# Attention values by seven block products, with a passage through DRAM to put them in order

## The chip, the cores and the metric

The kernel runs on one core of one Trainium2 chip. The metric is the device time of one execution in microseconds (us). Before the change the median of three runs is 2184.22 us (2183.15 to 2187.87).

## The reference

The input x has 2048 rows of 256 numbers. It is normalized by row, and the output is x plus an attention over 16 heads plus a gated feed-forward part whose weights are rounded to -1, 0 and 1. Everything is in 32-bit floats. What matters here is the attention:

```python
xn = _layernorm(x, axis=-1)
qkv = einsum('bsd,ed->bse', xn, Wqkv).reshape(B, S, 3 * H, D)   # H = 16, D = 128, S = 2048
q, k, v = qkv[:, :, :H], qkv[:, :, H:2 * H], qkv[:, :, 2 * H:]
logits = einsum('bqhd,bkhd->bhqk', q, k) * D ** (-0.5)
w = softmax(logits, axis=-1)
out = einsum('bhqk,bkhd->bqhd', w, v).reshape(B, S, H * D)
return einsum('bse,de->bsd', out, Wout)
```

## The kernel before

TensorE (PE) multiplies, ScalarE (ACT) takes the exponentials, VectorE (DVE) finds the maxima and reads products out of PSUM, GpSimd (POOL) does additions and subtractions in SBUF and issues part of the transfers; SyncE (SP) issues most of the others.

The normalized input lies transposed in SBUF as `xnT` (128 x 2 x 2048: two halves d of the 256 features, 2048 rows in four chunks of QB = 512). A loop over u goes through blocks of one head and 512 queries. There are 16 heads with NB = 4 blocks each, in 8 groups of G = 2 heads, so a group has GB = 8 blocks. Each block has TB = 4 quarters t of 128 queries. This text calls a pair of block i in its group and quarter t the slot (i,t); blocks 0 to 3 belong to the group's first head, 4 to 7 to its second; (8,t) is (0,t) of the next group. All engines carry out their instructions in the order in which the code issues them, so the place of a call in the loop is its place in each engine's queue.

In a slot, in order of issue, PE computes 128 x 2048 scores `s` for the query block that lies LEAD = 6 slots ahead (`scores`, in halves of 64 columns by `in_halves`, L94), then one product "beside" it (into the one PSUM bank of `ps_m`), then the weighted values of the current block (`weighted`, L716), and then, if the slot has one, a second product into the same bank. DVE reads the first product in the same slot, behind the maxima `mx`; it reads the second at the start of the next slot (`left`), behind the additions of weighted values to `oU` (`added`, L742, L746). In t = 2 and 3 of the running block the products are the block products for queries and keys of a later head (`pw`); in t = 0 and 1 they are output products of the group before (`pow`) while i < 4, and values of the group to come (`pvw`) while i >= 4. Before the change a value product (`v_product`) is 8 matmuls of 256 columns into one bank, for 256 rows of both heads, and there is no second product; `v_read` copies it with two DVE copies, rows in the partitions.

Queries and keys already come from seven products instead of eight: `weight_sums` and `x_sums` make sums of weight blocks and of chunks of x, `fast_product` multiplies them and `fast_read` combines the results. The chunks are taken in pairs, (0,1) and (2,3); `ts[0]` and `ts[2]` hold the four differences of a pair.

The weighted values too use fewer products. The exponentials are exchanged between partitions by DMA (`part<-p`), transposed by DVE into slots of `R` (`transposed`, L649), and POOL makes four differences T1 to T4 of them (`differences`, L669), some in halves: T1b and T3b at the start of t = 0, T2l at its end, T2h and T4 in t = 1, T1a and T3a of the next block in t = 3. `weighted` runs over k in four passes, one in each quarter: pass 0 in t = 0 takes `R` as it came, pass 1 takes T1 and T2 (T2l holds k < 4, T2h k >= 4), pass 2 T3, pass 3 T4, with half as many matmuls. The values have sums as well: `v_combined(h, 0)` and `(h, 1)` make two parts of `st` in the slot before a head's first block, `(h, 2)` and `(h, 3)` the others in its slot t = 1.

POOL's queue at the boundary of two blocks is: T1a and T3a (t = 3), `v_combined` 0 and 1 where a head begins, `put_away` (od<-oU, L772, waits for the finished `oU`), T1b, the transfer of the reciprocals (oT<-rd, L626), T3b, T2l, what `between` adds, T2h, T4. In t = 2 it issues rd<-r (L620). `between(n, t)` stands at the end of each slot and issues loads and transfers.

Of the kernel before, what the change touches and what calls it, by code (L numbers as in the profile page):

```python
# [9 lines left out]
F32 = mybir.dt.float32  # L10
F32R = mybir.dt.float32r
AF = mybir.ActivationFunctionType
ALU = mybir.AluOpType
# [7 lines left out]
def layernorm_attention_bitffn_kernel(  # L21
# [14 lines left out]
    nc = tc.nc  # L36
    P = 128
    S, DM = x.shape
    FF = w1T.shape[1]
    D = P  # L40
    HD = woutT.shape[0]
    H = HD // D
    KC = DM // P
    QB = 512
    NB = S // QB
    TB = QB // P
    NKT = S // P
# [3 lines left out]
    G = 2  # L51
# [18 lines left out]
    weights = {}  # L70
# [19 lines left out]
    def in_halves(out, lhs, rhs, start, stop, both=(True, True)):  # L90

        for c in range(2):
            if both[c]:
                nc.tensor.matmul(  # L94
                    out[c * HP : (c + 1) * HP], lhs[:, c * HP : (c + 1) * HP], rhs,
                    start=start, stop=stop, skip_group_check=True,
                )
# [47 lines left out]
    def weight_sums(h: int):  # L145
# [6 lines left out]
        nc.gpsimd.tensor_tensor(w[:, 3], wk[:, 1], w[:, 1], sub)  # L152
        ws[h] = w

    def x_sums(c: int):
        t = apool.tile([P, 4, QB], F32, tag=f"t{c}", name=f"t{c}", bufs=1)
        x00, x10 = (xnT[:, d, bass.ts(c, QB)] for d in range(KC))
        x01, x11 = (xnT[:, d, bass.ts(c + 1, QB)] for d in range(KC))
        for i, (a, b) in enumerate(((x01, x00), (x11, t[:, 0]), (x11, x01), (x10, t[:, 1]))):
            nc.gpsimd.tensor_tensor(t[:, i], a, b, ALU.subtract)  # L160
        ts[c] = t

    def fast_product(h: int, b: int, i: int, second: bool):

        c = b // 2 * 2
        wk, wq = (weights[h // G, i][:, :, bass.ts(h % G, D)] for i in "kq")
        w, t = ws[h], ts[c]
        x00, x10 = (xnT[:, d, bass.ts(c, QB)] for d in range(KC))
        x11 = xnT[:, 1, bass.ts(c + 1, QB)]
        lhs, rhs = {  # L170
            (0, 0): ((wk[:, 0], x00), (w[:, 1], t[:, 1])),
            (0, 1): ((w[:, 2], t[:, 2]), (wq[:, 1], t[:, 3])),
            (1, 0): ((w[:, 0], t[:, 0]), (w[:, 3], x11)),
            (1, 1): ((wk[:, 1], x10),),
        }[b % 2, i][second]
        pm = ps_m.tile([P, QB], F32, tag="m", name=f"pw{h}_{b}_{i}_{int(second)}")
        in_halves(pm, lhs, rhs, True, True)
        return pm

    def fast_read(h: int, b: int, i: int, second: bool, pm):  # L180
        c = b // 2 * 2
        if (b % 2, i) == (0, 0):
            if not second:
                if c == 0:
                    kTs[h] = kvpool.tile([P, S], F32, tag="kT", name=f"kT{h}")
                for j in range(2):
                    qTs[h, c + j] = kvpool.tile(
                        [P, QB], F32, tag="qT", name=f"qT{h}_{c + j}", bufs=NB + 2
                    )
        k0, k1 = (  # L190
            kTs[h].rearrange("p (j k r) -> p k j r", j=P // 32, r=32)[:, j * TB : (j + 1) * TB]
            for j in (c, c + 1)
        )
        q0, q1 = qTs[h, c], qTs[h, c + 1]
        pk = pm.rearrange("p (k j r) -> p k j r", j=P // 32, r=32)
        def q_sum(q, base):
            nc.vector.tensor_tensor(q, pm, base, ALU.add)  # L197

        def k_sum(k, base):
            nc.vector.tensor_tensor(k, pk, base, ALU.add)  # L200

        if (b % 2, i) == (0, 0):
            if not second:
                nc.vector.tensor_copy(k0, pk)
            else:
                k_sum(k1, k0)
        elif (b % 2, i) == (0, 1):
            if not second:
                nc.vector.tensor_tensor(
                    q1.rearrange("p (k j r) -> p k j r", j=P // 32, r=32), pk, k1, ALU.add  # L210
                )
            else:
                q_sum(q0, q1)
        elif (b % 2, i) == (1, 0):
            if not second:
                q_sum(q1, q1)
            k_sum(k1, k1)
        else:
            k_sum(k0, k0)
# [24 lines left out]
    def v_tile(h: int):  # L244

        if h == 1:
            return osums.rearrange("p b e (k d) -> p (b e k) d", d=D)
        if h not in vs:
            vs[h] = kvpool.tile([P, NKT, D], F32, tag="v", name=f"v{h}", bufs=3)
        return vs[h]  # L250
# [7 lines left out]

    def v_product(g: int, m: int, second: bool):
        w = weights[g, "v"]
        pm = ps_m.tile([P, 2, G * D], F32, tag="m", name=f"pvw{g}_{m}")
        for j in range(2):
            for d in range(KC):
                in_halves(
                    pm[:, j], xnT[:, d, bass.ts(2 * m + j, P)], w[:, d], d == 0, d == KC - 1
                )
        return pm

    def v_read(g: int, m: int, second: bool, pm):
        for j in range(G):
            nc.vector.tensor_copy(
                v_tile(g * G + j)[:, 2 * m : 2 * m + 2], pm[:, :, bass.ts(j, D)]
            )

    ppool = ctx.enter_context(tc.tile_pool(name="ppool", bufs=2))
    front = ExitStack()
# [7 lines left out]
    ods = [  # L286
        [away.tile([P, G, QB], F32, tag=f"od{g}_{c}", name=f"od{g}_{c}") for c in range(NB)]
        for g in range(2)
    ]
    rds = [away.tile([P, 32], F32, tag=f"rd{i}", name=f"rd{i}") for i in range(2)]  # L290

# [393 lines left out]
    def v_combined(h: int, i: int):  # L685
        ((l11, l12), (l21, l22)), st, s3 = v_parts(h)
        o, x, y, op = (
            (st[:, 0], l21, l22, ALU.add), (st[:, 1], st[:, 0], l11, ALU.subtract),
            (s3, l11, l21, ALU.subtract), (st[:, 2], l12, st[:, 1], ALU.subtract),
        )[i]  # L690
        nc.gpsimd.tensor_tensor(o, x, y, op)
# [87 lines left out]
    def o_fetched(g: int, b: int):  # L779
        nc.gpsimd.dma_start(o3, ods[g % 2][b])  # L780
# [86 lines left out]
    GB = G * NB  # L867
# [7 lines left out]
    def between(n: int, t: int):  # L875

        g, i = divmod(n, GB)
        last = NBK - NB

        if t == 1:  # L880
            if i == NB - 1 and g + 1 < H // G:
                load_weights(g + 1, "v", nc.gpsimd)
            elif i == GB - 1 and n < last or n == last - 1:
                load_weights(g, "o", nc.gpsimd)
        if g and i < NB:
            if t == 0 and i + 1 < NB:
                y_moved(i + 1, False)
            elif t == 1 and i + 1 < NB:
                o_fetched(g - 1, i + 1)
        elif n < last:  # L890
            if (i, t) == ((GB - 2, 2) if g else (GB - 1, 2)):
                y_moved(0, False)
            if (i, t) == (GB - 2, 3):
                o_fetched(g, 0)
        if n >= last - 1 and t == (1 if n < last else 2):
            b = n + 1 - last
            nc.gpsimd.dma_start(o3[:, b % 2], ods[(H - 2) // G % 2][b][:, 0])
        if (n, t) in ((last - 2, 3), (last - 1, 2)):
            fetched_back(n + 2 - last)
        if t == 0 and n in (last - 3, last - 2, last, last + 1):  # L900
            x_fetched((last - 3, last - 2, last, last + 1).index(n))

    behind = []
    with tc.manual_schedule():
        for u in range(-LEAD, (NBK - 1) * TB):
# [13 lines left out]
            if n >= NB and t < 2:  # L919
                i, j = divmod(i, NB)  # L920
                j = 2 * j + t
                if not i:
                    seven, hi = True, (g - 1, j)
                    product, read, twice = o_product, o_read, False
                elif g + 1 < H // G:
                    seven, hi = True, (g + 1, j)
                    product, read, twice = v_product, v_read, False
            pms = []

            def beside():  # L930
# [10 lines left out]
            if t == 0 and n >= 0:  # L941
                if 0 < n <= NBK - NB:
                    put_away(n - 1)
                differences(n, "T1b")
                spread(n)
                differences(n, "T3b")
            elif t == 1 and n >= 0:
                differences(n, "T2h")
                if blocks[n][1] == 0:
                    v_combined(blocks[n][0], 2)  # L950
                    v_combined(blocks[n][0], 3)
                differences(n, "T4")
            elif t == 3 and -1 <= n < NBK - 2:
                differences(n + 1, "T1a")
                if n % GB < NB <= n < NBK - NB - 2:
                    y_moved(n % GB, True)
                differences(n + 1, "T3a")
                if n >= 0 and blocks[n + 1][1] == 0:
                    v_combined(blocks[n + 1][0], 0)
                    v_combined(blocks[n + 1][0], 1)  # L960
            if more:
# [117 lines left out]
```

## Time and profile before

| | before |
|---|---|
| median of three runs | 2184.22 us |
| profiled execution | 2184.97 us |
| its span | 2183.2 us |
| PE busy, share of the span | 2160.2 us, 99% |
| DVE | 1725.5 us, 79% |
| ACT | 1374.6 us, 63% |
| POOL | 1472.0 us, 67% |
| granted PE clock, mean | 0.998 |
| value products pvw on PE | 896 matmul records, 117.7 us |
| block products pw<-t,ws on PE | 336 matmul records, 105.3 us |
| value copies on DVE (L273) | 112 of 128x256, 417 ns each |
| transfers of 512 KB by POOL, to landing | o<-od 4.2, osums<-yd 4.3, yd<-osums 3.4, ya<-in_x_dram 6.3 us |

Times in the views are us from the start of the span. Busy times leave out DMA-issuing instructions. The span of 2183.2 us and the time of the profiled execution differ by 1.8 us. A PE instruction of the program appears as two matmul records, and the two halves of 64 columns run side by side, so that lengths on PE are best read from the start of one stretch to the start of the next. In the timeline a line merges equal instructions that follow each other; in brackets stands the idle time before and what ended it.

### The profile page before, as it was taken

Reading aid. Unit: us, or ns where it says so; the run is one execution under the profiler, and the core shown is the slowest. Engines: PE = TensorE matmul, PEld = TensorE weight load, DVE = VectorE, ACT = ScalarE, POOL = GpSimd, SP = SyncE. Lnnn points to the kernel's source line nnn. Section 1 sums busy time; section 2 is a strip of 40 time slices with the busy share of each in tenths; the row PEclk is TensorE's granted clock in tenths of the full one; section 3 lists DMA queues with packets and bytes.
Section 4 is the critical chain, followed back from the end, with each engine's and each line's share of the span. In section 5 each row is a group of like instructions: output and inputs, shape, how many; then the busy total and the mean of one; then the engine's idle time right before and its main releaser. Section 6 shows DMA issues by size and latency. Waiting matters only on the chain. (4 is left out here: it accounts for less than half of the span.)

```text
span 2183.2 us, 41234 instructions
## 1 busy us (share of the span) xinstructions
PE 2160.2 (99%) x14074; PEld 1412.8 (65%) x14074; DVE 1725.5 (79%) x2338; ACT 1374.6 (63%) x2414; POOL 1472.0 (67%) x884
## 2 busy tenths in 40 slices
PE   9998999999999999999999999999999999999998
PEld 6744567776666666666666666666666665666665
DVE  6567887888887887888788788788788878888774
ACT  5586666666666666666666666666666666666662
POOL 0067767767667766767777776786766777677772
PEclk9999999999999999999999999999999999999999
DMA  2155545665556655566555654566555665556652
GB/s 93 41 115 138 124 112 136 159 170 134 120 138 164 163 129 124 142 170 156 122 135 143 175 144 113 135 159 172 130 118 138 173 160 126 126 141 175 168 144 80
DMA packets 180771, 300.65 MB, mean 138 GB/s; under 512 B 54416, under 2 KB 59920, under 8 KB 180560
## 3 DMA queue, kind: packets, MB, share of 16 engines
q1 hardware_dynamic: 127472, 174.69, 31.7%
q0 software_dynamic: 27152, 88.30, 15.9%
q10 hardware_dynamic: 25936, 35.03, 6.4%
q8 instruction: 111, 1.82, 0.4%
q14 instruction: 100, 0.82, 0.1%
HBM read 61.93 MB, written 34.54 MB: 44 GB/s over the span
## 5 line engine op out<-in xcount | busy, mean ns | idle before, releaser
L669 POOL TENSOR_TENSOR R<-R 128x1024 f32<-128x1024 f32 x441 | 1176.6, 2679 | 115.5 <-DVE R L649 100.4
L94 PE MATMUL s<-kT,qT 128*64 128x512 f32 x4000 | 953.2, 593 | 2.1 <-ACT p L578 2.1
L605 ACT COPY part<-p 32x512 f32<-32x512 f32 x1024 | 630.7, 616 | 394.8 <-issue 269.9
L568 DVE TENSOR_REDUCE mx<-s 128x1 f32<-128x1024 f32 x512 | 620.6, 1222 | 300.7 <-PE s L94 287.1
L94 PEld LDWEIGHTS s<-kT,qT 128*64 128x64 f32 x4000 | 502.9, 137 | 308.5 <-issue 80.9
L578 ACT ACTIVATE p<-s,nm 128x1024 f32<-128x1024 f32 x512 | 565.9, 1110 | 209.1 <-PE pw L94 105.7
L649 DVE STREAM_TRANSPOSE R<-part 128x1024 f32<-128x1024 f32 x512 | 605.2, 1220 | 15.1 <-DMA part<-p 13.1
L716 PE MATMUL av<-R,v 128*64 128x256 f32 x3728 | 551.0, 379 | 0.1
L716 PE MATMUL av<-R,st 128*64 128x256 f32 x3024 | 471.7, 379 | 11.0 <-POOL R L669 9.0
L716 PEld LDWEIGHTS av<-R,v 128*64 128x64 f32 x3728 | 363.4, 137 | 160.3 <-issue 8.8
L716 PEld LDWEIGHTS av<-R,st 128*64 128x64 f32 x3024 | 304.2, 137 | 97.3 <-POOL R L669 13.0
L620 POOL DMA_DIRECT2D rd<-r x60 | 33.7, 562 | 233.9 <-DVE r L619 233.9
L734 ACT COPY oU<-av 64x256 f32<-64x256 f32 x248 | 90.7, 366 | 127.0 <-PE av L716 124.6
L772 POOL DMA_DIRECT2D od<-oU x60 | 34.0, 567 | 195.1 <-DVE oU L746 192.6
L742 DVE TENSOR_TENSOR oU<-av,oU 64x256 f32<-64x256 f32 x248 | 102.2, 412 | 45.5 <-ACT oU L734 42.8
L94 PE MATMUL pvw<-wv,xnT 128*64 128x256 f32 x896 | 117.7, 379 | 0.0
L94 PE MATMUL pow<-o,wo 128*64 128x512 f32 x448 | 116.1, 592 | 0.0
L94 PEld LDWEIGHTS pvw<-wv,xnT 128*64 128x64 f32 x896 | 78.6, 137 | 42.3 <-DVE qT L197 5.2
L94 PE MATMUL pw<-t,ws 128*64 128x512 f32 x336 | 105.3, 592 | 0.0
L578 ACT ACTIVATION_READ_ACCUMULATOR p<-s,nm 128x1 f32 x512 | 100.3, 196 | 0.0
L94 PEld LDWEIGHTS pow<-o,wo 128*64 128x64 f32 x448 | 58.9, 137 | 37.3 <-issue 5.4
L200 DVE TENSOR_TENSOR kT<-pw,kT 128x512 f32<-128x512 f32 x112 | 76.9, 686 | 1.7
(146 smaller groups left out, 1332.2 us busy)
## 6 DMA issues: line engine op xcount, KB each, us to landing
part<-p SPq DMA_DIRECT2D x2552, 64.0 KB, 2.2
part<-p ACTq DMA_DIRECT2D x520, 64.0 KB, 2.1
oT<-rd POOLq DMA_DIRECT2D x60, 256.0 KB, 5.6
od<-oU POOLq DMA_DIRECT2D x60, 256.0 KB, 2.7
o<-od POOLq DMA_DIRECT2D x28, 512.0 KB, 4.2
osums<-yd POOLq DMA_DIRECT2D x28, 512.0 KB, 4.3
yd<-osums POOLq DMA_DIRECT2D x26, 512.0 KB, 3.4
yd<-yT SPq DMA_DIRECT2D x4, 512.0 KB, 2.6
```

The costliest lines, as they stand in the source:

```text
L94: nc.tensor.matmul(out[c * HP : (c + 1) * HP], lhs[:, c * HP : (c + 1) * HP], rhs, start=start, stop=stop, skip_group_check=True,)
L200: nc.vector.tensor_tensor(k, pk, base, ALU.add)
L568: nc.vector.tensor_reduce(mx[:, i : i + 1], s, AX.X, ALU.max)
L578: nc.scalar.activation(p, s, AF.Exp, bias=nm, scale=SCALE, accum_out=sums[n][:, t, i : i + 1],)
L605: nc.scalar.copy(*ends(j, j))
L620: nc.gpsimd.dma_start(rds[n % 2], riT)
L649: nc.vector.transpose(to[:, t % 2, 2 * i : 2 * i + 2], part.rearrange("p g (s c) -> p g s c", s=2),)
L669: nc.gpsimd.tensor_tensor(o, x, y, ALU.subtract)
L716: nc.tensor.matmul(av[i * HP : (i + 1) * HP, half], l[:, kk], moving(s, kk), start=start, stop=(k == units[r] - 1), skip_group_check=True,)
L734: nc.scalar.copy(u[op, oq], av[ap, half])
L742: nc.vector.tensor_tensor(u[p, q], av[p, half], u[p, q], ALU.add)
L772: nc.gpsimd.dma_start(ods[h // G % 2][b][:, h % G], oU)
```

## The change

The values of the groups 1 to 7 are made by seven block products for each half of the rows, in the way of the queries and keys. The two heads of the group take the places of query and key weights. `v_sums` makes four sums of weight blocks on POOL. `fast_v_product` gives 2 products of 512 columns in each slot with t = 0 or 1, i >= 4, but one in (5,1) and (7,1): 14 in a group. `fast_v_read` combines them on DVE: 16 operations on 128 x 512.

The results have features in the partitions and have to be transposed. For each head and half (1024 rows) `v_sent` writes 512 KB to DRAM in one transfer, `v_landed` brings it back in one, in pieces of 1 KB and with its blocks of 32 partitions exchanged, into a part of `xnT`, and `v_transposed` turns the 32 x 32 blocks by two DVE transposes of 512 elements a partition. `v_steps` puts these into `between`. For the part of `xnT` to be free, the chunks of the second pair change their parts: `pair(2)` is (3, 2) instead of (2, 3), in the products of queries and keys too.

`v_combined` 0 and 1 of a group's first head move from their place after T3a in (7,3) to the end of that slot, behind the last `v_transposed`.

```diff
+    def pair(c: int):
+        return (c, c + 1) if c == 0 else (c + 1, c)
+
     def x_sums(c: int):
         t = apool.tile([P, 4, QB], F32, tag=f"t{c}", name=f"t{c}", bufs=1)
-        x00, x10 = (xnT[:, d, bass.ts(c, QB)] for d in range(KC))
-        x01, x11 = (xnT[:, d, bass.ts(c + 1, QB)] for d in range(KC))
+        c0, c1 = pair(c)
+        x00, x10 = (xnT[:, d, bass.ts(c0, QB)] for d in range(KC))
+        x01, x11 = (xnT[:, d, bass.ts(c1, QB)] for d in range(KC))
...
-    def v_product(g: int, m: int, second: bool):
...
-    def v_read(g: int, m: int, second: bool, pm):
...
+    def v_sums(g: int):
+        wv = weights[g, "v"]
+        sums_of(wv[:, :, D:], wv[:, :, :D], f"wvs{g}")
+
+    def sums_of(k, q, name: str):
+        w = wpool.tile([P, 4, D], F32, tag="wx", name=name)
+        nc.gpsimd.tensor_tensor(w[:, 0], q[:, 0], q[:, 1], ALU.add)
+        nc.gpsimd.tensor_tensor(w[:, 1], w[:, 0], k[:, 0], ALU.subtract)
+        nc.gpsimd.tensor_tensor(w[:, 2], k[:, 0], q[:, 0], ALU.subtract)
+        nc.gpsimd.tensor_tensor(w[:, 3], k[:, 1], w[:, 1], ALU.subtract)
+        wxs[name] = w
+
+    def fast_v_product(g: int, m: int, second: bool):
+        half, m = divmod(m, NB)
+        wv, w, t = weights[g, "v"], wxs[f"wvs{g}"], ts[2 * half]
...
+        lhs, rhs = (
+            ((wv[:, 0, D:], x00), (w[:, 1], t[:, 1])),
+            ((w[:, 2], t[:, 2]), (wv[:, 1, :D], t[:, 3])),
+            ((w[:, 0], t[:, 0]), (w[:, 3], x11)),
+            ((wv[:, 1, D:], x10),),
+        )[m][second]
+        pm = ps_m.tile([P, QB], F32, tag="m", name=f"pvw{g}_{half}_{m}_{int(second)}")
+        in_halves(pm, lhs, rhs, True, True)
         return pm
...
+    def fast_v_read(g: int, m: int, second: bool, pm):
...
+        if (m, second) == (0, False):
+            nc.vector.tensor_copy(k0, pm)
+            return
+        todo = {
+            (0, True): ((k1, k0),), (1, False): ((q1, k1),), (1, True): ((q0, q1),),
+            (2, False): ((q1, q1), (k1, k1)), (2, True): ((k1, k1),), (3, False): ((k0, k0),),
+        }[m, second]
+        for o, i in todo:
+            nc.vector.tensor_tensor(o, pm, i, ALU.add)
+
+    def v_sent(h: int, half: int):
+        v = v_half(h, half).rearrange("p k d -> p (k d)")
+        nc.gpsimd.dma_start(
+            vds[h % G][half].rearrange("(r q) x -> q r x", q=P // 32), v
+        )
+
+    def v_landed(h: int, half: int):
+        nc.gpsimd.dma_start(landing, vds[h % G][half].rearrange("p (j c) -> j p c", j=P // 32))
+
+    def v_transposed(h: int, half: int):
+        v = v_half(h, half).rearrange("p k (q r) -> p q k r", r=32)
+        w = landing.rearrange("p (q k r) -> p q k r", q=P // 32, r=32)
+        for u in range(2):
+            nc.vector.transpose(v[:, 2 * u : 2 * u + 2], w[:, 2 * u : 2 * u + 2])
+
+    wxs, landing = {}, xnT[:, 0, QB : 3 * QB]
...
     def between(n: int, t: int):
...
+        v_steps = {
+            (5, 1): [(v_sent, 0, 0)], (5, 2): [(v_landed, 0, 0)],
+            (5, 3): [(v_transposed, 0, 0), (v_sent, 1, 0)],
+            (6, 1): [(v_landed, 1, 0)], (6, 2): [(v_transposed, 1, 0)],
+            (7, 1): [(v_sent, 0, 1)], (7, 2): [(v_landed, 0, 1)], (7, 3): [(v_transposed, 0, 1)],
+            (8, 1): [(v_sent, 1, 1)], (8, 2): [(v_landed, 1, 1)], (8, 3): [(v_transposed, 1, 1)],
+        }
...
+        for late in range(2):
+            if late < g + 1 < H // G + late:
+                for do, j, half in v_steps.get((i + late * GB, t), ()):
+                    do((g + 1 - late) * G + j, half)
+        if t == 3 and i == GB - 1 and g + 1 < H // G:
+            v_combined((g + 1) * G, 0)
+            v_combined((g + 1) * G, 1)
...
+        if t == 3:
+            if i == NB - 1 and g + 1 < H // G:
+                v_sums(g + 1)
...
-                    product, read, twice = v_product, v_read, False
+                    product, read, twice = fast_v_product, fast_v_read, j % NB != NB - 1
...
-                if n >= 0 and blocks[n + 1][1] == 0:
+                if n >= 0 and (n + 1) % GB == NB:
                     v_combined(blocks[n + 1][0], 0)
                     v_combined(blocks[n + 1][0], 1)
```

More of the change, by code (lines that the diff above doesn't have):

```diff
@@ L167, in fast_product @@
         w, t = ws[h], ts[c]
-        x00, x10 = (xnT[:, d, bass.ts(c, QB)] for d in range(KC))
-        x11 = xnT[:, 1, bass.ts(c + 1, QB)]
+        c0, c1 = pair(c)
+        x00, x10 = (xnT[:, d, bass.ts(c0, QB)] for d in range(KC))
+        x11 = xnT[:, 1, bass.ts(c1, QB)]
         lhs, rhs = {
@@ L191, in fast_read @@
             kTs[h].rearrange("p (j k r) -> p k j r", j=P // 32, r=32)[:, j * TB : (j + 1) * TB]
-            for j in (c, c + 1)
+            for j in pair(c)
         )
-        q0, q1 = qTs[h, c], qTs[h, c + 1]
+        q0, q1 = (qTs[h, j] for j in pair(c))
         pk = pm.rearrange("p (k j r) -> p k j r", j=P // 32, r=32)
@@ L255, in v_place @@
         return (k + NKT // 2) % NKT if h == 1 else k
-    def v_product(g: int, m: int, second: bool):
[L262 to L268, printed above, removed]
-        return pm
-    def v_read(g: int, m: int, second: bool, pm):
-        for j in range(G):
-            nc.vector.tensor_copy(
-                v_tile(g * G + j)[:, 2 * m : 2 * m + 2], pm[:, :, bass.ts(j, D)]
-            )
+    def v_sums(g: int):
+        wv = weights[g, "v"]
+        sums_of(wv[:, :, D:], wv[:, :, :D], f"wvs{g}")
@@ new lines, in sums_of @@
+    def sums_of(k, q, name: str):
[8 more added lines that the diff above has]
+        wv, w, t = weights[g, "v"], wxs[f"wvs{g}"], ts[2 * half]
+        c0, c1 = pair(2 * half)
+        x00, x10 = (xnT[:, d, bass.ts(c0, QB)] for d in range(KC))
+        x11 = xnT[:, 1, bass.ts(c1, QB)]
+        lhs, rhs = (
[6 more added lines that the diff above has]
+        in_halves(pm, lhs, rhs, True, True)
+        return pm
@@ new lines, in v_half @@
+    def v_half(h: int, half: int):
+        return v_tile(h)[:, half * NKT // 2 : (half + 1) * NKT // 2]
+    def fast_v_read(g: int, m: int, second: bool, pm):
+        half, m = divmod(m, NB)
+        q, k = (
+            v_half(g * G + i, half).rearrange("p k d -> p (k d)").rearrange(
+                "p (j k r) -> p k j r", j=P // 32, r=32
+            )
+            for i in range(G)
+        )
+        k0, k1, q0, q1 = (
+            i[:, j % 2 * TB : (j % 2 + 1) * TB] for i in (k, q) for j in pair(2 * half)
+        )
+        pm = pm.rearrange("p (k j r) -> p k j r", j=P // 32, r=32)
+        if (m, second) == (0, False):
[7 more added lines that the diff above has]
+            nc.vector.tensor_tensor(o, pm, i, ALU.add)
@@ new lines, in v_sent @@
+    def v_sent(h: int, half: int):
+        v = v_half(h, half).rearrange("p k d -> p (k d)")
+        nc.gpsimd.dma_start(
+            vds[h % G][half].rearrange("(r q) x -> q r x", q=P // 32), v
+        )
+    def v_landed(h: int, half: int):
[5 more added lines that the diff above has]
+            nc.vector.transpose(v[:, 2 * u : 2 * u + 2], w[:, 2 * u : 2 * u + 2])
@@ L288, in layernorm_attention_bitffn_kernel @@
         for g in range(2)
+    ]
+    vds = [
+        [away.tile([P, S // 2], F32, tag=f"vd{h}{i}", name=f"vd{h}{i}") for i in range(2)]
+        for h in range(G)
     ]
```

## The prediction

> **What bounds the kernel now.** I read the page first: its span, the busy time by engine, and the chain that ended last.
>
> ```profile
> span 2183.2 us, 41234 instructions
> PE 2160.2 (99%) x14074; PEld 1412.8 (65%) x14074; DVE 1725.5 (79%) x2338; ACT 1374.6 (63%) x2414; POOL 1472.0 (67%) x884
> PE 1%; DVE 0%; issue 0%; ACTq 0%; ACT 0%; DVEq 0%
> ```
>
> PE is busy for 99% and the chain names only the tail, so the set time is the matmul stream, provided it never waits. The busy time by engine of block 6 of one group (it begins at 907 us) confirms it: PE is busy for all of its 32.71 us, as it is in blocks 4, 5, 7 and 8.
>
> ```profile
> core 0: us, PE busy (x) PEld busy (x) DVE busy (x) ACT busy (x) POOL busy (x), PEclk, DMA share, GB/s
> 1100.40:1133.11 32.71, 32.71 (x228) 21.52 (x226) 26.65 (x36) 21.38 (x39) 23.20 (x16) 1.00 0.54 136
> ```
>
> So a saved matmul is worth its full time, and so is every wait the change makes for PE. The waits of PE say who comes closest:
>
> ```profile
> PE av L716 <- POOL R L669: 9.0, 8, 3.3
> ```
>
> Next, the PE timeline. A slot (i,t) is block i of the group, quarter t; (8,0) is (0,0) of the next group. Slots (6,1), (6,3) and (7,0):
>
> ```profile
> 1112.45 2.10 PE L94 MATMUL pvw<-wv,xnT 128*64 128x256 f32 x16
> 1114.17 3.82 PE L716 MATMUL av<-R,st 128*64 128x256 f32 x32
> ...
> 1126.23 3.80 PE L94 MATMUL s<-kT,qT 128*64 128x512 f32 x16
> 1129.66 1.23 PE L94 MATMUL pw<-t,ws 128*64 128x512 f32 x4
> 1130.52 2.10 PE L716 MATMUL av<-R,v 128*64 128x256 f32 x16
> 1132.25 1.23 PE L94 MATMUL pw<-t,wq 128*64 128x512 f32 x4
> ...
> 1136.54 2.10 PE L94 MATMUL pvw<-wv,xnT 128*64 128x256 f32 x16
> 1138.27 3.82 PE L716 MATMUL av<-R,v 128*64 128x256 f32 x32
> ```
>
> Lengths are taken from start to start: scores 3.43 (1126.23 to 1129.66), a value product 1.73 (1136.54 to 1138.27), one block product pw 0.86 (1129.66 to 1130.52), weighted values 1.73 in t=3 and twice that elsewhere.
>
> **What PE saves.** Per group 8 value products of 1.73 become 14 block products, whose shape is that of pw: 13.84 - 14 x 0.86 = **1.80 us**, or 12.6 us in 7 groups. Nearly all of it falls in (5,1) and (7,1), where there is no second product. But the product ahead of the weighted values falls from 1.73 to 0.86 in every slot with t=0 or 1, and the second one stands behind them: those matmuls now come **0.87 us earlier in their slot**.
>
> **What this meets on POOL.** The weighted values of t=1 read in their first half (k<4) what difference T2l writes, and in their second half, 1.73 us later, what T2h writes. Both end a POOL chain that starts when DVE has finished the previous block's oU. Block 6:
>
> ```profile
> 1103.07 0.69 DVE L746 TENSOR_TENSOR oU<-oU,oT 128x512 f32<-128x512 f32 x1
> 1104.05 0.56 POOL L772 DMA_DIRECT2D od<-oU  x1 [3.92 <-DVE oU L746]
> 1112.37 2.35 POOL L669 TENSOR_TENSOR R<-R 128x1024 f32<-128x1024 f32 x1
> ```
>
> The od issue starts 0.29 us after oU ends at 1103.76; T2h (third line) ends at 1114.72. PE needs it at 1114.17 + 1.73 = 1115.90. A slack of 1.18 us becomes 0.31 by the 0.87 above. In block 4 T2h ends at 1050.2 for a need at 1051.36: 1.16 becomes 0.29. In blocks 5 and 7 the slack is about 2 us and stays above 1. In block 8 the o product (1.73) stays, and the slack is 0.57 us (need 1180.45, T2h ends at 1179.88). A POOL end reaches PE after some 0.09 us: in (2,1) of the same group T2h ended at 986.88 and PE, which waited, went on at 986.97.
>
> Now the additions, each where it stands, per group.
>
> *v_sums in (3,3).* Four 128x128 additions on POOL, like the four ws (1119.32 to 1121.13, 1.81 us), just ahead of the od issue of (4,0), which has 0.86 us of idle time before it. So od and T2h come 0.95 us late: 0.95 - 0.29 + 0.09 = **0.75 us** of PE wait in (4,1).
>
> *v_transposed in (5,3).* Two transposes of 512 elements on DVE. Two of 1024 take 2.36 us (below), so I take half of it with an end overhead: 1.22. Its transfer back, issued at about 1093.7 behind rd, has until 1102.5. DVE does not idle between there and the reads of (6,0):
>
> ```profile
> 1100.21 2.36 DVE L649 STREAM_TRANSPOSE R<-part 128x1024 f32<-128x1024 f32 x2
> 1102.60 0.43 DVE L742 TENSOR_TENSOR oU<-av,oU 64x256 f32<-64x256 f32 x1
> 1103.79 2.36 DVE L568 TENSOR_REDUCE mx<-s 128x1 f32<-128x1024 f32 x2
> ```
>
> The first read of (6,0), now 0.68 us, starts at 1106.31 + 1.22 and ends at 1108.21; the second product, due at 1100.40 + 3.44 + 0.86 + 3.46 = 1108.16, waits 0.14 for the one bank. od and T2h are late by 1.22: 1.22 - 0.31 - 0.14 + 0.09, about 0.8 us in (6,1). Together **0.95 us**.
>
> *v_transposed in (6,2).* Its v_landed stands on POOL behind T4 and ws, so with the 1.22 it is issued at about 1122.3. DVE has done its own transposes at 1126.60 + 0.95 = 1127.55. The transfer is 512 KB from DRAM in 1 KB pieces; the rows are
>
> ```profile
> osums<-yd POOLq DMA_DIRECT2D x28, 512.0 KB, 4.3
> ...
> ya<-in_x_dram POOLq DMA_DIRECT2D x4, 512.0 KB, 6.3
> ```
>
> between 4.3 (long pieces) and ya's largest, 7.6. I take 6.3, because ya has the same size, queue and piece length. Then it lands at 1128.6, DVE waits 1.1 us and transposes to 1129.9, and behind it are queued two oU additions (0.85) and the read of (6,2)'s second product (0.61), on which the first product of (6,3) waits: due at 1130.6, it starts at 1131.5 (0.9 us). Maxima and read follow; the second product, only 1.73 us behind here, waits 0.55 more. **1.45 us**. If it lands by 4.3, 0.25 us is left (that slot has almost no slack now: its read ends at 1132.14, the product starts at 1132.25); at 7.6, 2.75.
>
> [...]
>
> *v_transposed and v_combined in (7,3).* Two st sums (2.63 us with their gap) move on POOL from before DVE's end of block 7 to behind the transposes; od follows:
>
> ```profile
> 1164.65 1.27 POOL L691 TENSOR_TENSOR st<-v 128x512 f32<-128x512 f32 x1
> 1166.00 1.28 POOL L691 TENSOR_TENSOR st<-st,v 128x512 f32<-128x512 f32 x1
> 1168.61 0.58 POOL L772 DMA_DIRECT2D od<-oU  x1 [1.33 <-DVE oU L746]
> ```
>
> DVE ends its transposes at 1167.1, and v's at 1168.35; the sums run to 1171.1, and od starts there instead of at 1168.61: 2.5 us late. 2.5 - 0.57 + 0.09, about **2.05 us** in (8,1).
>
> *Without a term of their own.* The other v_landed of (7,2) and (8,2) are issued some 8 us ahead of the transposes. The v_sent (0.56 us each, as yd) stand in POOL's idle time ahead of rd (3 to 6 us), except in (5,3) and (8,1), where od (idle 3.9) and rd follow late enough; without that cover each would put 0.56 on od. v_landed in (8,2) waits for v_sent's landing and holds T1a 1.3 us, which has until (9,1). The 14 more DVE reads (16 of about 0.61 us for 16 of 0.34) fall in t=1 and 2, where DVE idles over 2 us, or in (5,0) and (7,0), where they still end before the second product. The (8,3) transposes take (9,1)'s slack of 1.4 us down to about 0.2. The exchange of the second pair's parts adds no instruction.
>
> [...]
>
> **Sum.** Waits 0.75 + 0.95 + 1.45 + 2.05 = 5.20 us; less 1.80: **+3.40 us per group**, +23.8 in 7. The profiled execution was 2184.97 us (span 2183.2 and 1.8 around it) and would become 2208.8; from the median of 2184.2 I get **2208.0 us**.
>
> **Rivals.** *The POOL and DVE chains have room that I misjudge* (they start earlier where PE has waited, and the waits vanish): the product saving alone stands, 2184.2 - 12.6 = 2171.6. For it: PE loses nothing today. Against: the slacks of 0.3 and 0.57 us are read from the trace. It decides from the point where all waits stay under 1.8 us per group, less than the one in (8,1). Chance 0.12. *Only (8,1) waits:* 2.05 - 1.80 = +0.25 per group, 2186. It needs v_sums and both transposes hidden. 0.06. *The transfers crowd the exchange of the parts:* the queues are 52 to 54% busy in these blocks, and each half adds 1 MB. If every one of the 28 returns lands 2 us later still, past DVE's arrival, that is 28 x 1 to 2 us more: 2236 and above. Against: blocks 0 to 3 carry three such transfers each and PE never waits for a part there. 0.12.
>
> **Range and chances.** The forecast has 0.70. Its own bounds: with half of the waits (2.6) +0.8 per group, 2190; with the slow landing (+1.3) and a 1 us wait at another one, +5.7, 2224. That leaves out the first rival, the crowding one and part of the second, about 0.2. What a measurement can tell from no change is 0.2%, 4.4 us. Faster 0.12, same 0.06, slower 0.82.
>
> **What would show it.** PE busy falls by about 12 us, yet its waits for POOL R grow from 9 to 30 us or so, most in (8,1), whose slot goes from 8.60 to about 10.7; (4,1) and (6,1) to 9.4; (6,3) from 6.88 to 8.3; (5,1) and (7,1) fall to 7.75. v_landed lands in about 6.3. It is wrong if those slots stay at 8.60, or if (6,3) shows no wait of DVE for a transfer.

## The result, and the profile after

The changed kernel takes 2530.67 us (median of 5 runs, 2525.63 to 2537.83) against 2186.08 us before on the same chip: a ratio of 1.1577, 95% interval 1.1555 to 1.1599. The sign of the forecast was right; its size of 1% was not: the loss is 345 us, more than fourteen times the 23.8 forecast.

The page of the changed kernel, with the rows of the transfers that the prediction had to size:

```profile
span 2536.1 us, 40375 instructions
PE 2229.6 (88%) x13570; PEld 1253.6 (49%) x13570; DVE 1794.4 (71%) x2394; ACT 1378.2 (54%) x2414; POOL 1554.3 (61%) x968
vd<-v POOLq DMA_DIRECT2D x28, 512.0 KB, 11.5
xnT<-vd POOLq DMA_DIRECT2D x28, 512.0 KB, 12.9
yd<-osums POOLq DMA_DIRECT2D x26, 512.0 KB, 3.4
ya<-in_x_dram POOLq DMA_DIRECT2D x4, 512.0 KB, 5.9
```

The last column is the median time from issue to landing. The sending, which the prediction likened to yd (3.4 us) without writing down a landing of its own, takes 11.5; the return, which it put beside ya (6.3), takes 12.9. The rows it compared with have hardly moved: yd 3.4 as before, ya 5.9 for 6.3, osums 5.0 for 4.3. The waits, each with who waited for whom, the total, the count and the longest:

```profile
DVE v L335 <- DMA xnT<-vd: 290.8, 28, 14.7
PE av L783 <- DVE oU L809: 110.4, 14, 8.8
PE pow L94 <- DVE qT L202: 103.2, 7, 15.5
PE pw L94 <- DVE kT L205: 57.8, 7, 9.9
PE av L783 <- POOL R L736: 16.0, 22, 3.3
```

The first line is the cause and the next three are its effects on PE: every one of the 28 `v_transposed` (L335) stands on DVE waiting for its return, 10.4 us on average, and PE waits for what is queued behind it. One such place is (6,0). The three views show first POOL, then DVE, then PE:

```profile
1237.18 0.75 POOL L324 DMA_DIRECT2D vd<-v  x1
1242.81 0.57 POOL L687 DMA_DIRECT2D rd<-r  x1 [4.88 <-DVE r L686]
1250.24 1.61 POOL L329 DMA_DIRECT2D xnT<-vd  x1 [6.87 <-DVE kT L205]
```

```profile
1250.72 2.37 DVE L716 STREAM_TRANSPOSE R<-part 128x1024 f32<-128x1024 f32 x2 [0.72 <-DMA part<-p]
1262.09 1.30 DVE L335 STREAM_TRANSPOSE v<-xnT 128x512 f32<-128x512 f32 x2 [9.01 <-DMA xnT<-vd]
1263.43 0.43 DVE L809 TENSOR_TENSOR oU<-av,oU 64x256 f32<-64x256 f32 x1
```

```profile
1255.26 1.03 PE L94 MATMUL pvw<-xnT,wv 128*64 128x512 f32 x4
1263.91 6.25 PE L783 MATMUL av<-R,v 128*64 128x256 f32 x32 [7.62 <-DVE oU L809]
1269.99 1.02 PE L94 MATMUL pvw<-t,wvs 128*64 128x512 f32 x4
```

The sending leaves at 1237.18. The return is next in POOL's queue behind rd and goes out at 1250.24, 13.1 us after the sending. The view puts the 6.87 us of idle time before it down to DVE, but the sending's last 4 KB packet ends only at 1249.28: it is the landing of vd that ends there. The return lands at about 1262.1; DVE waits 9.01 us, and only then adds the weighted values that free PE's bank. PE waits 7.62 us.

Slot lengths, taken from the starts of the scores on PE, say where the time stands. The numbers are means of groups 1 to 6; all other slots keep their length within 0.1 us:

| slot | before | after | difference |
|---|---|---|---|
| (4,1), (8,1) | 8.64, 8.60 | 9.29, 9.40 | +0.65, +0.80 |
| (4,3), (8,3) | 6.91, 6.88 | 7.10, 7.10 | +0.18, +0.22 |
| (5,1), (7,1) | 8.61 | 7.75 | -0.87 each |
| (6,0) | 8.61 | 20.56 | +11.95 |
| (6,3) | 6.88 | 17.74 | +10.87 |
| (8,0) | 8.60 | 19.17 | +10.56 |
| (9,0) | 8.60 | 25.76 | +17.16 |

Together +50.6 us per group, 354 in 7, close to the difference of the two spans (352.9). Each of the four returns costs one slot 10.6 to 17.2 us.

### The profile page after: what moved, and what is told of

Same layout as the page of the kernel before. It is cut to its first block, busy times and chain, and to the rows that moved or that the text cites. A ratio compares the mean times of both kernels' runs of the same rounds, so it can differ in the third digit from the quotient of the medians.

```text
span 2536.1 us, 40375 instructions
## 1 busy us (share of the span) xinstructions
PE 2229.6 (88%) x13570; PEld 1253.6 (49%) x13570; DVE 1794.4 (71%) x2394; ACT 1378.2 (54%) x2414; POOL 1554.3 (61%) x968
## 3 DMA queue, kind: packets, MB, share of 16 engines
q8 instruction: 107, 1.75, 0.3%
## 5 line engine op out<-in xcount | busy, mean ns | idle before, releaser
L94 PE MATMUL s<-kT,qT 128*64 128x512 f32 x4000 | 939.1, 592 | 7.1 <-ACT p L645 6.8
L783 PE MATMUL av<-R,v 128*64 128x256 f32 x3728 | 584.9, 406 | 102.5 <-DVE oU L809 102.3
L94 PEld LDWEIGHTS s<-kT,qT 128*64 128x64 f32 x4000 | 393.0, 137 | 435.2 <-issue 341.3
L783 PEld LDWEIGHTS av<-R,v 128*64 128x64 f32 x3728 | 383.7, 148 | 279.7 <-DVE oU L809 114.3
L783 PE MATMUL av<-R,st 128*64 128x256 f32 x3024 | 478.6, 383 | 18.1 <-POOL R L736 16.0
L335 DVE STREAM_TRANSPOSE v<-xnT 128x512 f32<-128x512 f32 x56 | 36.5, 690 | 290.8 <-DMA xnT<-vd 290.8
L329 POOL DMA_DIRECT2D xnT<-vd x28 | 44.8, 1599 | 152.8 <-DMA vd<-v 121.9
L94 PEld LDWEIGHTS pow<-o,wo 128*64 128x64 f32 x448 | 39.6, 147 | 167.8 <-DVE qT L202 111.5
L94 PEld LDWEIGHTS pw<-t,ws 128*64 128x64 f32 x336 | 36.5, 143 | 90.2 <-issue 84.7
## 6 DMA issues: line engine op xcount, KB each, us to landing
vd<-v POOLq DMA_DIRECT2D x28, 512.0 KB, 11.5
xnT<-vd POOLq DMA_DIRECT2D x28, 512.0 KB, 12.9
```

What stands on the lines that cost most here:

```text
L94: nc.tensor.matmul(out[c * HP : (c + 1) * HP], lhs[:, c * HP : (c + 1) * HP], rhs, start=start, stop=stop, skip_group_check=True,)
L329: nc.gpsimd.dma_start(landing, vds[h % G][half].rearrange("p (j c) -> j p c", j=P // 32))
L335: nc.vector.transpose(v[:, 2 * u : 2 * u + 2], w[:, 2 * u : 2 * u + 2])
L783: nc.tensor.matmul(av[i * HP : (i + 1) * HP, half], l[:, kk], moving(s, kk), start=start, stop=(k == units[r] - 1), skip_group_check=True,)
```

## The experiments

Four theories could explain a landing of 11 to 13 us. Theory A: a transfer written with 4 as its outermost count is carried by 4 of the 16 DMA engines. Theory B: the memory is slow at these addresses (rows 16 KB apart) or pieces (1 KB). Theory C: POOL is slow to make the descriptors. Theory D: the exchange of the parts crowds the transfers.

The packet records speak for A before any run: where a sending had the POOL queue to itself (the 128 packets of 4 KB issued at 1237.18), 3.7 packets were in flight on average from 3 to 8 us after the issue, and never more than 5. Most of them took 0.159 us, as in the 512 KB transfers of before, where 18 to 20 overlap at the peak.

**Four transfers instead of one**, at the same addresses:

```diff
-        nc.gpsimd.dma_start(vds[h % G][half].rearrange("(r q) x -> q r x", q=P // 32), v)
+        to = vds[h % G][half].rearrange("(r q) x -> q r x", q=P // 32)
+        for q in range(P // 32):
+            nc.gpsimd.dma_start(to[q], v[bass.ts(q, 32)])
...
-        nc.gpsimd.dma_start(landing, vds[h % G][half].rearrange("p (j c) -> j p c", j=P // 32))
+        to = landing.rearrange("p (q c) -> p q c", q=P // 32)
+        src = vds[h % G][half].rearrange("(r q) (j c) -> j r q c", q=P // 32, j=P // 32)
+        for j in range(P // 32):
+            nc.gpsimd.dma_start(to[bass.ts(j, 32)], src[j])
```

> Same bytes to the same addresses as the changed kernel, but each transfer is cut along its outer count of 4: four transfers of 32 partitions (128 KB) out and four back. Theory A (a transfer whose outermost count is 4 is carried by only 4 of the 16 DMA engines, so 512 KB takes 11.5 us out and 12.9 us back): the last of four lands within 3 to 5 us, DVE's wait of 290.8 us for the landed half shrinks to under 40 us, and the time falls from 2530 to 2195 to 2230. Theory B (the memory is slow at rows 16 KB apart, or at pieces of 1 KB): the addresses are the same, so it stays near 2530. Theory D (the exchange of the parts crowds the transfers): the same traffic, stays above 2450.

Measured: 2219.51 us, ratio 1.0150 (1.0105 to 1.0196), and

```profile
vd<-v POOLq DMA_DIRECT2D x112, 128.0 KB, 3.6
xnT<-vd POOLq DMA_DIRECT2D x112, 128.0 KB, 3.5
```

Same bytes, same addresses, same pieces, same neighbours: 311 of the 345 us are gone, and DVE's idle time before the transposes falls from 290.8 us to 8.0. B and D fall. What changed is the outermost count, now 32, and with it the size and the number of the transfers; the next run and the one cut in two tell these apart.

**Plain rows both ways:** `dma_start(vds[h % G][half], v)` and `dma_start(landing, vds[h % G][half])`, outermost count 128. This leaves out the exchange of the blocks.

> One transfer out and one back, both as plain 128 rows of 4 KB; the exchange of the blocks of 32 partitions is left out, so the values are in the wrong order. Theory A: 128 rows spread over all engines, out in about 3.4 us and back in about 4.3 us (the rows of yd and osums), time near 2200 by the slot sums of the prediction (+2.2 us per group with a landing of 4.3). Theory B gives the same here. Theory D: the same bytes beside the same exchange, so landing stays above 9 us and the time above 2450.

Measured: 2206.68 us, ratio 1.0090 (1.0070 to 1.0110); single transfers of 512 KB land in 4.0 and 4.7 us. So neither the size nor the single transfer is what is slow.

**No transfers.** `v_sent` and `v_landed` return at once.

> No transfer out or back at all (the transposes read what lies in the landing place, so the values are wrong); products, reads, sums and transposes stay. The prediction's slot sums without the wait for a landing: -1.80 + 0.75 + 0.95 + 0.25 + 2.05 = +2.2 us per group, 2200; (4,1) and (6,1) near 9.4, (8,1) near 10.7 us. The rival that the transfers are the whole loss and the POOL and DVE chains have room: 2172. If the loss sits elsewhere (the transposes or products themselves): above 2300.

Measured: 2206.70 us, ratio 1.0086 (1.0063 to 1.0109). The transfers as the change has them are thus worth 324 of the 345 us, and the plain ones of the run above cost nothing beside that. The rest is the four POOL and DVE terms of the prediction, and some that it missed. The slots give (4,1) +0.68 (the median; one group has +2.3), (6,0) +0.14, (6,1) +0.46, (6,3) +0.27, (8,1) +1.75, (9,0) +1.08, (4,3) and (8,3) +0.2 each, less 1.74 in (5,1) and (7,1).

**Issued by SP:** `nc.sync` in place of `nc.gpsimd` in both.

> The changed kernel's single transfers, issued by SP instead of POOL. Theory A: still 4 engines, so landings stay at 10 to 13 us, and the time stays above 2450 (SP's queue may add waits for the exchange of the parts). Theory C (POOL makes the descriptors slowly, its issue took 1.6 us): landings fall below 5 us and the time below 2300.

Measured: 2617.64 us. The waits:

```profile
DVE v L335 <- DMA xnT<-vd: 366.7, 28, 17.5
```

No faster from another queue (13.1 us a wait instead of 10.4), so C falls. The page gives no landing for transfers that SP issues, but the packets speak for A again. SP's queue (q1) in the changed kernel and in this one, with packets, MB and the share of 16 engines:

```profile
q1 hardware_dynamic: 127472, 174.69, 27.9%
q1 hardware_dynamic: 145616, 204.05, 31.1%
```

That is 18144 packets more. The data of the 28 halves, 128 packets of 4 KB out and 512 of 1 KB back for each, make 17920; 224 are left, 4 for each of the 56 transfers. They are packets of 4 bytes, and every other transfer on this queue has 16 of them (41136 for 2571). If each of them stands for one engine that takes part, that is 4 engines against 16; no record names the engine of a packet, so this is a reading of the counts. The packets in flight fit it: the 128 of a sending take 7.0 to 10.2 us with about 3.1 in flight, while the 128 packets of yd<-yT, 512 KB on the same queue, take 1.4 us with 14.4 in flight.

**Cut in two, outermost count 2:** `dma_start(to[q : q + 2], v[q * 32 : q * 32 + 64])` for q = 0 and 2, and the same for the return, issued by POOL.

> The changed kernel with each transfer cut in two of 64 partitions, outermost count 2. Theory A in its strict form (the outermost count is the number of DMA engines): each of the two is carried by 2 engines; 64 packets of 4 KB on 2 engines at the 0.159 us of a packet are at least 5 us each beside the other traffic, so the last one lands as late as the single transfer or later (10 to 20 us), and the time stays above 2450. Rival (any transfer of 64 partitions or fewer spreads well, the size of 512 KB is what is slow): landing under 5 us, time near 2220.

Measured: 2608.01 us (one run).

```profile
vd<-v POOLq DMA_DIRECT2D x56, 256.0 KB, 11.3
xnT<-vd POOLq DMA_DIRECT2D x56, 256.0 KB, 13.3
```

Half the size takes the same time; with a count of 32 a quarter of the size takes a third of it (3.6 and 3.5 us), and with 128 the whole size takes about as little (4.0 and 4.7 us). In these runs the count decides, not the size. In most sendings the two together keep 3 to 4 packets in flight, so, if theory A holds, the second one does not share the first one's pair of engines. POOL's transfers carry the count in their packets too: those under 512 bytes rise by 400 a transfer with a count of 4 (22400 for 56) and by 464 with a count of 2 (51968 for 112), but by 16 with 32 or 128. 400 is 16 and 12 times 32, and 464 is 16 and 14 times 32, 32 being, by theory A, the data packets on each engine that carries any (128 on 4, 64 on 2). It looks as if each of the other 12 or 14 engines got 32 small ones. In the sending issued at 1237.18, 396 of its 400 packets of 4 bytes, 12 times 33, end by 1239.13, the other four between 1247.84 and 1249.50, at the end of the data. The reading is argued from these numbers alone.

The runs with counts of 2, 4, 32 and 128 agree: A is what is left. What they show is the time to landing at each count, for the sending and the return: 11.3 and 13.3 us with 2 (256 KB each), 11.5 and 12.9 with 4 (512 KB), 3.6 and 3.5 with 32 (128 KB), 4.0 and 4.7 with 128 (512 KB). That the count limits the number of engines is read from the packets.

**All steps placed anew.** Out in one plain transfer, back in four. Each step stands where the engine it burdens idles, and the two `v_combined` are back in their old place behind T3a:

```diff
         v_steps = {
-            (5, 1): [(v_sent, 0, 0)], (5, 2): [(v_landed, 0, 0)],
-            (5, 3): [(v_transposed, 0, 0), (v_sent, 1, 0)],
-            (6, 1): [(v_landed, 1, 0)], (6, 2): [(v_transposed, 1, 0)],
-            (7, 1): [(v_sent, 0, 1)], (7, 2): [(v_landed, 0, 1)], (7, 3): [(v_transposed, 0, 1)],
-            (8, 1): [(v_sent, 1, 1)], (8, 2): [(v_landed, 1, 1)], (8, 3): [(v_transposed, 1, 1)],
+            (5, 1): [(v_sent, 0, 0), (v_sent, 1, 0)], (5, 2): [(v_landed, 0, 0)],
+            (6, 1): [(v_transposed, 0, 0), (v_landed, 1, 0)],
+            (7, 0): [(v_sent, 0, 1)],
+            (7, 1): [(v_transposed, 1, 0), (v_sent, 1, 1), (v_landed, 0, 1)],
+            (7, 2): [(v_transposed, 0, 1)],
+            (8, 2): [(v_landed, 1, 1)], (9, 1): [(v_transposed, 1, 1)],
         }
...
-        if t == 3:
+        if t == 2:
             if i == NB - 1 and g + 1 < H // G:
                 v_sums(g + 1)
```

> Same products; out in one plain transfer of 128 rows, back in four of 32 partitions; v_sums a quarter earlier, behind rd in (3,2), where POOL idles; every v_transposed at the end of a quarter t = 1 or, once, 2, behind which DVE waited over 2 us for scores; the two v_combined back in their old place. If the rest of the loss in the kernels without slow transfers is what the slots show (POOL late by v_sums in (4,1), by v_transposed in (6,1), by the moved v_combined in (8,1), the one bank in (6,3) and (9,0)), each of these slots returns to 8.60 (6,3: 6.88) and the time is the product saving alone, 2186 - 12.6 = 2173.5, with up to 1 us per group left: 2172 to 2181. Rival (seven products cost PE or DVE more than counted): 2190 or above.

Measured: 2191.76 us, ratio 1.0026 (1.0017 to 1.0035): above the range expected, at the number of the rival. The rival's reason does not hold, though: (5,1) and (7,1) take 7.75 us, as counted. (8,1) and (9,0) are at their lengths of before in every group, (4,1), (6,1) and (6,3) in nearly all (single groups are up to 1.3 us longer; why is open). One slot is not, (7,3) with 8.47 instead of 6.02 us. Its cause is the only wait for a return that is left:

```profile
DVE v L336 <- DMA xnT<-vd: 14.1, 7, 3.1
```

**v_sums left at the end of (3,3)**, all else as above.

> The kernel with all steps placed anew, but v_sums where the change has it, at the end of (3,3). The prediction's term: 0.75 us in (4,1) per group, so 5 us over the kernel with v_sums earlier, and (4,1) at 9.3 instead of 8.60. Rival (POOL has room there): same time, (4,1) at 8.60.

Measured: 2200.24 us, ratio 1.0066 (1.0052 to 1.0079), 8.5 us over the kernel above; (4,1) takes 9.37 us in most groups, so +0.77 where 0.75 was forecast, and (4,3) another 0.2, which was not. Together 6.8 us in 7 groups; 5 were expected.

**The return in (7,1) issued first**, ahead of the other sending and the load of wo:

```diff
-            (7, 1): [(v_transposed, 1, 0), (v_sent, 1, 1), (v_landed, 0, 1)],
+            (7, 1): [(v_transposed, 1, 0), (v_landed, 0, 1), (v_sent, 1, 1)],
```

with the loop over `v_steps` in `between` put ahead of the loads, which moves the other steps of the loop ahead of them too.

> As the kernel with all steps placed anew, with one landing place, but the return in (7,1) is issued ahead of the load of wo and of the other sending: 1.3 us earlier. DVE's wait of 1.7 us in (7,2) falls to about 0.4, (7,3) to about 7.1, the time to about 2182. If POOL's queue position does not matter: 2191.8 again.

Measured: **2174.73 us, ratio 0.9947 (0.9934 to 0.9961)**, better than expected: (7,3) takes 6.13 us, and no wait of DVE for a return is left. The wait was expected to fall to about 0.4 us; why it vanished is open. The kernel is faster than the one before by 0.5%.

```profile
span 2170.7 us, 40501 instructions
PE 2147.3 (99%) x13570; PEld 1431.2 (66%) x13570; DVE 1783.9 (82%) x2394; ACT 1375.1 (63%) x2414; POOL 1561.8 (72%) x1052
1000.00:1260.00 260.00, 260.00 (x1668) 180.27 (x1666) 222.01 (x293) 166.34 (x292) 200.65 (x137) 1.00 0.62 162
```

The last line, from the busy time by engine in a stretch, shows PE busy for all of 260 us. What the products save is read from (5,1) and (7,1): 0.87 us less in each, 12.2 us in 7 groups, where 12.6 was counted. PE's busy time is 12.9 us below that of before, but it is a rougher measure: the next version, with the same products, has 2155.1 us, only 5.1 below.

**A second landing place.** The second head's first half lands in another buffer, `o3`, and the return of (7,1) goes out between T2h and T4.

> As the kernel with all steps placed anew, and the last wait removed: there DVE waited 1.7 us in (7,2) for the return of the first head's second half, which could be issued only when the one landing place was free, and (7,3) took 8.47 instead of 6.02 us. Here the second head's first half lands in the idle buffer o3 (o_fetched waits until (7,1)), and the return in question is issued between T2h and T4 of (7,1), some 4.5 us earlier. If that wait was all that was left: (7,3) at 6.02 to 6.3, 7 x 2.4 = 17 us less than 2191.8, 2173 to 2177, below the kernel before by 0.4 to 0.6%. Rival (DVE's 1.22 us of transposes alone carry over into (7,3) and (8,1)): 2180 to 2186.

Measured: 2177.33 us, ratio 0.9952 (0.9938 to 0.9965); (7,3) at 6.13 as in the version above, so nothing was left for it to gain; the two cannot be told apart.

**The first head's second half as in the change**, all else as in the best version: transposed in (7,3), the two `v_combined` behind it.

> As the kernel with the return issued first in (7,1), but the first head's second half as the change has it: sent in (7,1), back in (7,2), transposed in (7,3), with the two v_combined of the group's first head behind that transpose instead of after T3a. The prediction's term for this: od of (8,0) starts 2.5 us late and PE waits 2.05 us in (8,1). So (8,1) near 10.6 instead of 8.60, and the time 14 us above 2174.7, 2186 to 2191. Rival (POOL catches up before T2l and T2h are needed): (8,1) at 8.60, time as before at 2175.

Measured: 2187.45 us, ratio 1.0008 (0.9998 to 1.0018), 12.7 us over the best version. (8,1) takes 10.41 us instead of 8.60, +1.81 where the prediction had 2.05, and (8,3) another 0.22, which it did not have: +2.03 per group. This term alone eats the whole gain of the products.

## Why the prediction was wrong

The step that failed is the time put for the transfers. The prediction put `v_landed` beside ya "because ya has the same size, queue and piece length", gave it bounds of 4.3 to 7.6 us from rows, and likened `v_sent` to yd. The runs show 12.9 and 11.5 us. Even the issue on POOL, put at 0.56 us "as yd", took 0.74 for the sending and 1.60 for the return. Size, queue and piece length were not what decides in these runs; the outermost count of the transfer as it was written was (4.0 and 4.7 us for 512 KB with 128), and the diff shows it (`-> q r x` and `-> j p c`, q and j counting 4). Every transfer that POOL issued before has 16 packets of 4 bytes (4880 for 305), as many as those with a count of 32 or 128 add, so by that mark none of the rows compared with was confined to fewer engines. Nothing in the prediction allowed for that.

With this one time all clauses that rested on it fell: that the returns of (5,2), (7,2) and (8,2) arrive ahead of the transposes, that the sending's landing holds POOL only in (8,2), and that only (6,2) has DVE waiting. The rival in which every return comes late was named, with 2236 us and above and a chance of 0.12. Its number covers 2530 only by "and above": it priced 2 us of lateness where the waits were 10.4 on average, and its mechanism, crowding by the parts, fell with the run of four transfers, which moves the same bytes beside the same parts. The shares that the prediction gave for that crowding, 52 to 54%, are too narrow a reading as well: its five windows of blocks 4 to 8 have 0.47 to 0.62. Of its signs, (5,1) and (7,1) came true; PE's busy time rose instead of falling, and (6,1) stayed at 8.60 in the changed kernel, where (6,0) had taken the longer wait.

The terms beside it, point by point, read on kernels without the slow transfers:

- *Products, -1.80 us per group.* Confirmed: (5,1) and (7,1) at 7.75, so -1.74 in these two.
- *v_sums in (4,1), 0.75.* 0.77, and 0.2 in (4,3) that had no term.
- *v_transposed in (5,3), 0.95.* 0.14 in (6,0) as forecast, 0.46 instead of 0.8 in (6,1): 0.60 without transfers. Why (6,1) waits less is open.
- *v_transposed in (6,2).* 0.27 without transfers, where 0.25 was forecast for an early landing; the 1.45 taken rested on the landing.
- *v_combined in (7,3), 2.05.* 1.81 in (8,1), and 0.22 in (8,3) that had no term. That the two add up to the forecast within 0.02 is luck.
- *The (8,3) transposes, no term.* Wrong by 1.08 us. The prediction looked at POOL's slack in (9,1) and overlooked the one bank: the output product of (9,0) waits until DVE has read the second product of (8,3). Before, the read and then the product, which does not wait:

```profile
1200.17 0.69 DVE L197 TENSOR_TENSOR qT<-pw,qT 128x512 f32<-128x512 f32 x1
1201.08 2.08 PE L94 MATMUL pow<-o,wo 128*64 128x512 f32 x8
```

In the kernel without transfers the read comes behind the transposes and the late oU:

```profile
1214.85 0.69 DVE L202 TENSOR_TENSOR qT<-pw,qT 128x512 f32<-128x512 f32 x1
1215.60 1.94 PE L94 MATMUL pow<-o,wo 128*64 128x512 f32 x8 [0.66 <-DVE qT L202]
```

The slots of the kernel without transfers add up to about +3.05 us per group, 21.4 in 7, and 19.3 was measured, so the slots account for the time. The forecast for that kernel by the prediction's own terms was +2.2 per group, 15.4 in 7: 4 us too low, with a term too high (v_transposed in (5,3)) against one left out ((9,0)). One row that was not of the same kind cost 324 us.

## What to carry to other kernels

Before sizing a transfer by another row, compare how both are written, above all the outermost count of both sides; 512 KB took 4 to 5 us with a count of 128 and 11 to 13 with 4. Where one engine is busy all the time, read for each added step which queue it stands in and what is next behind it: slots and slacks from the trace gave the costs that were looked for to 0.4 us or better, and one of 1.08 us was not looked for. And place a step where its engine waits anyway: with fast transfers in the slots of the change the kernel was 1.5% slower than before, in other slots 0.5% faster.

## What the runs showed that was not expected

The waits alone are not the whole loss. PE has about 12 us less to do in the changed kernel than before, yet its busy time is 2229.6 us, 82 above the 2147.3 of the best version with the same products. The windows of the busy time show most of the reason; the third number from the end is the granted clock of PE, as a share of full speed:

```profile
1250.10:1263.90 13.80, 4.88 (x23) 1.60 (x19) 4.11 (x6) 7.21 (x13) 7.01 (x4) 0.82 0.58 135
1263.90:1270.80 6.90, 6.89 (x36) 3.80 (x38) 6.31 (x8) 2.67 (x5) 5.88 (x4) 0.62 0.56 130
```

In the 6.9 us after a wait of 7.62 us the granted clock is 0.62 on average, and the pass of weighted values from 1263.91 takes 6.08 us to the next stretch instead of 3.46. The clock records of the trace have 0.5 from 1258.92, 2.6 us after PE's last matmul ended, until 1269.16, 5.3 us after PE went on, and 1.0 on either side. It is the same at each of PE's 28 waits behind a late return, 6.5 to 15.5 us long: the records have 0.5 from 2.1 to 5.4 us after PE's last matmul ended until 2.7 to 5.8 us after PE went on. In the profiled executions of the kernels without slow transfers the mean clock stayed at 0.995 or above, against 0.94 here. PE was idle for 306.5 us (span less busy time) against 23.0 before, 284 us more of waiting. Of the 82 us of busy time beside it, the lower clock explains about 67, an estimate: PE was busy for 137 us at half clock, against 3 in the best version, and half of the difference is lost if work takes twice as long there. The other 15 or so are open.
